# Own products paired with the routing, zero rows stored during the first aggregation, and the degrees' row made ahead of a branch, in a graph layer with experts

## Chip, cores and metric

One Trainium2 chip, of which the kernel uses one core. The metric is the device time in microseconds (us) of one execution. Before the change three executions took 2622.99, 2624.7 and 2629.7 us; the median is 2624.7 us.

## What is computed

`x` holds 6250 nodes of 256 features, `src` and `dst` hold 106,250 directed edges (50,000 drawn edges in both directions, and a loop for every node), sorted by `dst`. The reference, cut to what matters here:

```python
xn = layernorm(x)
def graph_conv(x, edges, W0, b0, W1, b1):        # every edge counts in both directions
    deg = maximum(segment_sum(ones, dst), 1)
    agg = segment_sum(x[src], dst) / deg[:, None]
    return x @ W0 + b0 + agg @ W1 + b1
h   = relu(graph_conv(xn, edges, W0_0, b0_0, W1_0, b1_0))     # 256 -> 512
gnn = graph_conv(h, edges, W0_1, b0_1, W1_1, b1_1)            # 512 -> 256
mix = linear_attention(xn, Wq, Wk, Wv, Wfc)   # k^T v per head, so one 256 x 256 matrix for all nodes
x   = x + gnn + mix
y   = layernorm(x)
top2, weights = top_k(y @ Wg + bg + bias, 2)                  # 8 experts
out = x + sum over the two experts e of weight * (relu(y @ W1[e] + b1[e]) @ W2[e] + b2[e])
```

Everything is float32 on the outside.

## The kernel before

**Tiling.** The nodes lie in `NB` = 49 blocks of 128. Four blocks are a group; there are `NGRP` = 13 groups, the last with one block. A neighbour sum is done as a product with an adjacency matrix: for each group of destination blocks and each source block `j`, a 128 x 512 tile of counts is multiplied with the normalized nodes `sent` (held in SBUF as two parts, a rounded one and the rest).

**Stages.** The kernel runs through five, one after the other; the times are those of the profiled execution.

1. 0 to 427 us: the edges are placed, that is, each edge gets a slot in a table `place` from which the adjacency tiles can be built by comparison. The nodes are normalized meanwhile.
2. 427 to 1172 us: the first aggregation (`aggregate`). VectorE makes one-hots (L667), TensorE multiplies them to adjacency tiles (L685), ScalarE takes these out of PSUM and adds up the degrees `degp` (L688), VectorE makes a bf16 copy `kept` (L695), SP stores it to `adjd` in DRAM (L696), and TensorE multiplies the tile with `sent` (L640). A unit is two tiles.
3. 1172 to 1190 us: the degrees are summed (L821), and the program takes a branch (`tc.If` at L727) that holds a slow path for edges which found no slot; with these inputs it isn't entered. Behind it, SP issues five loads (L860 to L862: transposed nodes and own products of group 0), and the row 1/degree is made: maximum and reciprocal (L864, L865), a transpose on TensorE (L867), a copy, a store of 24.5 KB to `rdeg_d` (L870). Then `mean(0)` reads it back, broadcast to all partitions (L877), and scales the aggregate `aggT` with it (L879).
4. 1190 to 1490 us: both dense products of the first convolution and the first part of the second.
5. From 1490 us: the second aggregation over the stored tiles with the gate behind each group, and from 2160 us the experts. These scatter and gather rows through the DRAM buffer `ybuf`, which has to be zero where no row is written.

**Order inside the first stage.** The order of TensorE's, VectorE's, ScalarE's and SP's instructions is that of the program text here (`manual_schedule`, L225): each of these engines works its own queue in order. Generators interleave the work. The main loop (L591) takes one batch `b` of four blocks (two pairs of blocks) after the other, 13 batches. In `assign(b)` a batch has

- ten rank groups: three matmuls (L380, L384, L389) into a PSUM tile `rk`, which VectorE reduces (L420); three tiles are in flight;
- a few small VectorE steps to `slot` (L439);
- for each of the two pairs, five `route` comparisons (L447) and four `carry` products (L456) on VectorE, with a yield behind each; then 38 routing matmuls (L469) and ScalarE's copies to `place` (L473 to L479), without a yield.

At each of its 31 yields, the batch advances `count(b + 1)` (the next batch's one-hots and running sums), `edges` (decoding of further edges), and, as long as a budget of `per_round` = 30 lasts, the generator `left`. `left` is the chain of `nodes(g)` for groups 2 to 12, and then `mixing()`. Groups 0 and 1 go first, ahead of the main loop (L579 to L583).

**`nodes(g)`** normalizes a group: statistics (L238, L241) on VectorE, a square root on ScalarE (`sd`, L246), its reciprocal on VectorE (L248), the normalization on ScalarE (L254) and the rounded part of `sent` (L257). Then eight transposes on TensorE (L264) give `xnT` (one buffer), which ScalarE copies out (L265) and stores to `xnT_d` (L267); VectorE subtracts for the second part of `sent` (L268). Next come the own products `xn @ W0_0`: four terms `f`, each of two matmuls (L273) into a PSUM tile `tp` (two buffers, shared with the transposes), an ACTIVATE with the bias (L276) and a store to `self_d` (L277), with a yield behind each term. The profile counts each float32 matmul as several records, so a term of a group of four blocks is four records of L273. Last comes `gram`, the sum of `xn^T xn` (L282), and the load of the group after the next (L286).

**`mixing()`** turns `gram` into the one 256 x 256 matrix of the attention. It begins with three weight loads on SP (L484) of which the first goes into `late`, the memory of the weights `W0_0` that the own products use, and a store of zeros to all of `ybuf` (L493, 13.4 MB in one DMA).

Of the kernel before, what the change touches and what calls it, by code (L numbers as in the profile page):

```python
# [8 lines left out]
F32 = mybir.dt.float32  # L9
# [3 lines left out]
AF = mybir.ActivationFunctionType  # L13
# [26 lines left out]
def tile_gps_layer(ctx: ExitStack, tc: tile.TileContext, a, out):  # L40
# [95 lines left out]
    with ExitStack() as p1:  # L136
# [90 lines left out]
        def load_nodes(g):  # L227
            load_rows(xns[g % XB][:, :, :D], blocks(g), nc.sync)

        def nodes(g):  # L230

            bs = blocks(g)
            n = len(bs)
            xn = xns[g % XB]
            st = wk.tile([P, T, nc.vector.BN_STATS_DIM], F32, name="st")
            mv = wk.tile([P, T, nc.vector.BN_AGGR_DIM], F32, name="mv")
            for i in range(n):
                nc.vector.bn_stats(st[:, i, :], xn[:, i, :D])  # L238
                yield
            for i in range(n):  # L240
                nc.vector.bn_aggr(mv[:, i, :], st[:, i, :])  # L241
                yield
            sd = wk.tile([P, T], F32, name="sd")
            rs = wk.tile([P, T], F32, name="rs")
            off = wk.tile([P, T], F32, name="off")
            nc.scalar.activation(sd[:, :n], mv[:, :n, 1], AF.Sqrt, bias=eps)  # L246
            yield
            nc.vector.reciprocal(rs[:, :n], sd[:, :n])  # L248
            yield
            nc.vector.scalar_tensor_tensor(off[:, :n], mv[:, :n, 0], -1.0, rs[:, :n], op0=OP.mult,  # L250
                                           op1=OP.mult)
            yield
            for i in range(n):
                nc.scalar.activation(xn[:, i, :D], xn[:, i, :D], AF.Identity, bias=off[:, i:i + 1],  # L254
                                     scale=rs[:, i:i + 1])
            part = sent[:, bs[0]:bs[-1] + 1]
            nc.scalar.copy(part[:, :, 0], xn[:, :n, :D])  # L257
            yield
            yield
            xnT = wk.tile([P, DC, T * P], F32, name="xnT", bufs=1)  # L260
            for c in range(DC):
                tp = pt1.tile([P, T * P], F32, name="tp")
                for i in range(n):
                    nc.tensor.transpose(tp[:, i * P:(i + 1) * P], xn[:, i, c * P:(c + 1) * P], ident)  # L264
                nc.scalar.copy(xnT[:, c, :n * P], tp[:, :n * P])  # L265
                yield
            nc.scalar.dma_start(xnT_d[:, :, bs[0] * P:(bs[-1] + 1) * P], xnT[:, :, :n * P])  # L267
            nc.vector.tensor_sub(part[:, :, 1], xn[:, :n, :D], part[:, :, 0].bitcast(F32))  # L268
            yield
            for f in range(FC):  # L270
                tp = pt1.tile([P, T * P], F32, name="tp")
                for c in range(DC):
                    nc.tensor.matmul(tp[:, :n * P], w00[:, c, f * P:(f + 1) * P],  # L273
                                     xnT[:, c, :n * P], start=(c == 0), stop=(c == DC - 1))
                own = (wq, wfc)[f % 2].rearrange("p c d -> p (c d)")
                nc.scalar.activation(own[:, :n * P], tp[:, :n * P], AF.Identity, bias=bh[:, f:f + 1])  # L276
                nc.scalar.dma_start(self_d[f, :, bs[0] * P:(bs[-1] + 1) * P], own[:, :n * P])  # L277
                yield

            for i, b in enumerate(bs):  # L280
                for c in range(DC):
                    nc.tensor.matmul(gram[:, GW[c]:GW[c] + W - c * P], xn[:, i, c * P:(c + 1) * P],  # L282
                                     xn[:, i, c * P:], start=False,
                                     stop=(b == NB - 1 and c == DC - 1))
                yield
            if g + XB < NGRP:  # L286
                load_nodes(g + XB)
# [125 lines left out]
        def assign(b):  # L413
# [25 lines left out]
            nc.vector.tensor_mul(flat(slot[:, :n]), rk, flat(fit))  # L439
            yield  # L440
            for i in range(n):
                routes = []
                for q0, q1 in QS:
                    nq = q1 - q0
# [36 lines left out]
        def mixing():  # L481


            for to, k in ((wkv, "WkvT"), (wq, "Wq"), (wfc, "WfcT")):  # L484
# [2 lines left out]
            x0, x1 = (xns[k].rearrange("p t w -> p (t w)") for k in range(2))  # L487
            b1p = x1[:, :NE * EC]
            nc.scalar.dma_start(b1p, a["b1e"].rearrange("p e c -> p (e c)"))

            none = x0[:, DC * W + D:DC * W + 2 * D]
            nc.vector.memset(none, 0.0)
            nc.sync.dma_start(ybuf.rearrange("(t p) d -> p t d", p=P),  # L493
                                            none[:, None, :].to_broadcast([P, TILES, D]))
            gs, m1 = (x0[:, :DC * n].rearrange("p (c d) -> p c d", c=DC) for n in (W, D))
            vk = x0[:, DC * W:DC * W + D].rearrange("p (c k) -> p c k", c=DC)
            gk, plain = x1[:, :DC * D].rearrange("p (c d) -> p c d", c=DC), x1[:1, DC * D:DC * D + 2 * D]
# [76 lines left out]
            for part in parts:  # L574
                yield from part

        EARLY = 2
        load_edges(PK * 2)
        for _ in nodes(0):  # L579
            pass  # L580
# [5 lines left out]
        for _ in count(0):  # L586
            pass
        load_edges(PK * 2)
        left = chained(*(nodes(g) for g in range(EARLY, NGRP)), mixing())
        per_round = -(-(NGRP - EARLY) * 30 // max(1, NBAT - 2))  # L590
        for b in range(NBAT):  # L591
            ahead_ = count(b + 1) if b + 1 < NBAT else iter(())
            k = b // (PK // PB) + 1
# [56 lines left out]
    def aggregate():  # L650

        with ExitStack() as s:
            hp = s.enter_context(tc.tile_pool(name="hots", bufs=4))
            ap = s.enter_context(tc.tile_pool(name="adj", bufs=4))
            pa = s.enter_context(tc.tile_pool(name="pa", bufs=4, space=PSUM))
            pg = s.enter_context(tc.tile_pool(name="pg", bufs=2, space=PSUM))
            s.enter_context(tc.manual_schedule(engines={ENG.PE, ENG.DVE, ENG.Activation}))
            hots, adjs, sums = {}, {}, {}
            units = [(g, js) for g in range(NGRP) for js in order_of(g)]

# [35 lines left out]
                nc.sync.dma_start(adjd[g, :, j, :n * P], kept[:, :n * P])  # L696

            AH, AB = 2, 1
            for u in range(len(units) + AH):
                if u < len(units):  # L700
                    g, js = units[u]
                    for j in js:
# [5 lines left out]
                if u >= AH:  # L708
# [8 lines left out]
                    if last:  # L717
                        n = len(blocks(g))
                        cols = slice(g * T * P, (g * T + n) * P)
                        nc.vector.tensor_copy(aggT[:, 0, cols], sums[g][0][:, :n * P])  # L720
                        nc.scalar.copy(aggT[:, 1, cols], sums[g][1][:, :n * P])

    def aggregate_any(first_conv):

# [2 lines left out]
        with tc.If(nc.values_load(misfit[0:1, 0:1], min_val=0, max_val=1) == 1), ExitStack() as s:  # L727
# [74 lines left out]
            for b in range(NB):  # L802
# [8 lines left out]
                else:  # L811
# [2 lines left out]
                    nc.vector.scalar_tensor_tensor(base, v[:, :D], rdeg[:, b:b + 1], base,  # L814
                                                   op0=OP.mult, op1=OP.add)
                    nc.sync.dma_start(btab[b * P:(b + 1) * P, :], base)
            if not first_conv:
                nc.vector.memset(rdeg, 0.0)

    aggregate()  # L820
    nc.vector.tensor_reduce(deg, degp, AX.X, OP.add)  # L821
    aggregate_any(True)
    ppool_ctx.__exit__(None, None, None)
    JL = 7
# [12 lines left out]
    with ExitStack() as p2:  # L837
# [22 lines left out]
        load_group(0)  # L860
        for f in range(FC):
            load_own(0, f)  # L862

        nc.vector.tensor_scalar(rdeg, deg, 1.0, None, op0=OP.max)  # L864
        nc.vector.reciprocal(rdeg, rdeg)  # L865
        pd = py.tile([P, 512], F32, name="pz")
        nc.tensor.transpose(pd[:NB, :P], rdeg, ident)  # L867
        rdT = wk.tile([P, T * P], F32, name="hT", bufs=6)[:NB, :P]
        nc.vector.tensor_copy(rdT, pd[:NB, :P])
        nc.sync.dma_start(rdeg_d.rearrange("(b p) -> b p", p=P), rdT)  # L870

        def mean(g):

            bs = blocks(g)
            cols = slice(bs[0] * P, (bs[-1] + 1) * P)
            rd = wk.tile([P, T * P], F32, name="rd", bufs=1)
            nc.sync.dma_start(rd[:, :len(bs) * P], bcast_rows(rdeg_d[cols], len(bs) * P))  # L877
            for c in range(DC):
                nc.vector.tensor_mul(aggT[:, c, cols], aggT[:, c, cols], rd[:, :len(bs) * P])  # L879

# [488 lines left out]
```

## Time and profile before

The profiled execution took 2623.89 us, of which 2622.1 us are the span from its first to its last instruction.

| | |
|---|---|
| median of three runs | 2624.7 us |
| profiled execution, its span | 2623.89 us, 2622.1 us |
| TensorE busy (matmuls) | 2418.6 us, 92% of the span |
| VectorE busy | 1605.2 us, 61% |
| ScalarE busy | 949.1 us, 36% |
| GpSimd busy | 343.5 us, 13% |
| granted TensorE clock, mean | 0.948 of full speed |
| DRAM traffic | 164.27 MB read, 159.95 MB written |

How such rows are read: "PE" is TensorE's matmuls, "PEld" its weight loads, "DVE" VectorE, "ACT" ScalarE, "SP" SyncE, which issues most of the DMAs; a "q" behind an engine's name is its queue of DMA issues, branches and the like. `L273` is line 273 of the kernel before. `tp<-xnT,late` says which tile is written from which. In a row of the timeline, the first number is the start and the second the duration in us, `x16` stands for 16 instructions of a kind in a row, and the bracket at the end gives how long the engine was idle before it and what ended that. In a list of waits, the waiting group stands left of the arrow and the one it waited for right of it.

### The profile page before, as it was taken

What the parts mean: (1) busy time and instruction counts of PE and PEld (TensorE: products, weight loads), DVE (VectorE), ACT (ScalarE), POOL (GpSimd) and SP (SyncE); (2) the same over time, 40 slices, a digit from 0 to 9 for tenths busy, and PEclk for the clock granted to TensorE, in tenths of its full rate; (3) what the DMA queues carried; (4) which work ended last, traced back from release to release, by engine and by line L of the source; (5) the groups of instructions that cost most, each with busy time, mean ns of one, the idle gap of its engine ahead of it and who ended that gap; (6) DMA issues with size and microseconds to landing.
All of it is one profiled execution on the core that took longest, in us unless ns stands there. A gap on an engine that the chain in (4) does not pass through costs nothing. (4 is left out here: it accounts for less than half of the span.)

```text
span 2622.1 us, 42322 instructions
## 1 busy us (share of the span) xinstructions
PE 2418.6 (92%) x13030; PEld 1828.8 (70%) x13030; DVE 1605.2 (61%) x4300; ACT 949.1 (36%) x2528; POOL 343.5 (13%) x372
## 2 busy tenths in 40 slices
PE   4788867999999999988999889999999968999998
PEld 2555545777777777776777778888888865777775
DVE  4888788888888888862333224444444434666666
ACT  2334313555555555541111123343343322333332
POOL 0000000000000000000000101211211212444444
PEclk9798877999999999998999999999999958999999
DMA  3222262333333333323333354554544442223333
GB/s 101 68 100 83 71 230 70 110 109 110 109 109 106 113 109 111 107 79 124 135 133 129 105 204 153 167 164 159 169 160 157 147 125 68 75 76 104 108 114 94
DMA packets 242754, 312.47 MB, mean 119 GB/s; under 512 B 53574, under 2 KB 202737, under 8 KB 242262
## 3 DMA queue, kind: packets, MB, share of 16 engines
q1 hardware_dynamic: 212690, 254.95, 30.3%
q0 software_dynamic: 16896, 33.80, 3.9%
q10 hardware_dynamic: 12932, 20.91, 2.2%
q8 instruction: 107, 1.75, 0.3%
q14 instruction: 129, 1.06, 0.1%
HBM read 164.27 MB, written 159.95 MB: 124 GB/s over the span
## 5 line engine op out<-in xcount | busy, mean ns | idle before, releaser
L640 PE MATMUL sum<-adj,sent 128*128 128x512 f32 (+1 forms) x5096 | 1258.2, 398 | 14.9 <-DVE adj L993 8.1
L640 PEld LDWEIGHTS sum<-adj,sent 128*128 128x128 f32 x5096 | 919.4, 193 | 194.2 <-DVE adj L993 8.5
L688 ACT ACTIVATE adj<-pt 128x512 fp32r<-128x512 f32 (+1 forms) x637 | 359.1, 570 | 348.5 <-PE pt L685 344.2
L667 DVE TENSOR_TENSOR oh<-iota,place 128x1024 bf16<-128x1024 bf16 (+1 forms) x686 | 404.1, 630 | 91.8 <-PE pt L685 89.7
L993 DVE CAST adj<-many 128x512 fp32r<-128x512 bf16 (+1 forms) x319 | 135.8, 427 | 321.8 <-PE sum L640 273.7
L991 ACT CAST adj<-many 128x512 fp32r<-128x512 bf16 (+1 forms) x318 | 188.6, 594 | 389.4 <-PE sum L640 346.8
L695 DVE CAST kept<-adj 128x512 bf16<-128x512 f32 (+1 forms) x637 | 235.9, 406 | 16.0 <-DMA adjd<-kept 6.9
L685 PEld LDWEIGHTS <-oh 128*128 128x128 bf16 x2548 | 148.1, 98 | 84.8 <-DVE kept L695 63.6
L1271 PEld LDWEIGHTS po<-w2e,hT 128*128 128x128 f32 x840 | 159.7, 190 | 67.3 <-issue 25.2
L685 PE MATMUL pt<-oh 128*128 128x128 bf16 x2548 | 204.7, 221 | 1.6 <-DVE oh L667 1.0
L1251 PE MATMUL pm<-w1e,yT 128*128 x420 | 201.3, 602 | 1.3 <-DMA row<-lists 1.3
L1271 PE MATMUL po<-w2e,hT 128*128 x840 | 198.6, 379 | 1.1 <-ACT hT L1263 1.1
L1275 ACT ACTIVATE res<-res,row 128x256 f32<-128x256 f32 x105 | 53.3, 508 | 301.6 <-DVE res L1274 301.6
L952 POOL IOTA home_i<- 128x8 int32 x1 | 0.1, 129 | 1063.6 <-SPq L727 1063.6
L1130 POOL DMA_INDIRECT lists<-rows,place_i x98 | 97.2, 992 | 305.9 <-DVE rows L1122 248.5
L1307 POOL DMA_INDIRECT out_dram<-both,at x105 | 106.8, 1017 | 175.2 <-DVE both L1305 165.9
L688 ACT ACTIVATION_READ_ACCUMULATOR adj<-pt 128x1 f32 x637 | 126.4, 198 | 0.0
L469 PE MATMUL rt<-carry,route 128*128 128x100 bf16 x931 | 68.5, 240 | 60.2 <-DVE carry L456 39.9
L1292 POOL DMA_INDIRECT got<-ybuf,at x105 | 108.2, 1031 | 69.3 <-issue 33.0
L1254 DVE TENSOR_TENSOR hb<-pm,b1c 128x512 f32<-128x512 f32 x105 | 72.6, 692 | 63.9 <-PE pm L1251 63.3
L1251 PEld LDWEIGHTS pm<-w1e,yT 128*128 128x128 f32 x420 | 72.7, 193 | 53.8 <-issue 52.0
L469 PEld LDWEIGHTS <-route 128*128 128x128 bf16 x931 | 61.3, 116 | 69.2 <-issue 59.0
(255 smaller groups left out, 2575.4 us busy)
## 6 DMA issues: line engine op xcount, KB each, us to landing
adjd<-kept SPq DMA_DIRECT2D x588, 128.0 KB, 1.8
many<-adjd SPq DMA_DIRECT2D x84, 896.0 KB, 4.6
row<-lists SPq DMA_DIRECT2D x105, 130.5 KB, 2.1
ybuf<-xn SPq DMA_DIRECT2D x1, 13440.0 KB
ybuf<-res SPq DMA_DIRECT2D x105, 128.0 KB, 2.0
hT<-self_d SPq DMA_DIRECT2D x48, 256.0 KB, 5.3
xn<-in_x_dram SPq DMA_DIRECT2D x12, 512.0 KB, 3.9
xnT_d<-xnT ACTq DMA_DIRECT2D x12, 512.0 KB, 3.2
```

What stands on the lines that cost most here:

```text
L469: nc.tensor.matmul(pl[:, r], routes[q // 4][:, q % 4, :, r], carry[:, q - q0, :, :, r], start=(q == 0), stop=(q == Q - 1))
L640: nc.tensor.matmul(sums[g][c][:, :n * P], sent[:, j, k, c * P:(c + 1) * P], adj[:, :n * P], start=(first and k == 0), stop=(last and k == 1))
L667: nc.vector.tensor_tensor(oh, iota2[:, None].to_broadcast([P, m, P, 2]), place[:, j, v0:v0 + m, None, :].to_broadcast([P, m, P, 2]), op=OP ...
L685: nc.tensor.matmul(cols, o[:, :, r], o[:, :, 1 - r], start=(m == 0), stop=(m + 1 == len(todo)))
L688: nc.scalar.activation(adj[:, :n * P], pt[:, :n * P], AF.Copy, accum_out=degp[:, j, g:g + 1])
L695: nc.vector.tensor_copy(kept[:, :n * P], adjs[g, j][:, :n * P].bitcast(F32))
L991: nc.scalar.copy(adj[:, :n * P], from_)
L993: nc.vector.tensor_copy(adj[:, :n * P], from_)
L1251: nc.tensor.matmul(pm, yT[:, c], w1e[:, bass.ds(e, 1), c, :].rearrange("p o f -> p (o f)"), start=(c == 0), stop=(c == DC - 1))
L1271: nc.tensor.matmul(po, hT[:, f], w2e[:, bass.ds(e, 1), f, :].rearrange("p o d -> p (o d)"), start=(f == 0), stop=(f == EC - 1))
L1292: ga = nc.gpsimd.indirect_dma_start(out=gots[t % 4], out_offset=None, in_=ybuf, in_offset=bass.IndirectOffsetOnAxis(ap=outs[t][1][:, 0:1], ...
L1307: st = nc.gpsimd.indirect_dma_start(out=out, out_offset=bass.IndirectOffsetOnAxis(ap=at[:, 1:2], axis=0), in_=both, in_offset=None, bounds ...
```

## The change

Four edits.

1. **Own products.** `nodes(g)` no longer multiplies a group's own products. It puts its four terms into a queue `owed`; `own_term` takes one term out and issues its matmuls, its ACTIVATE and its store. `assign` calls it twice ahead of each pair of blocks, so four times a batch. Since `xnT` has one buffer, terms that are still owed are done ahead of the next group's transposes. Groups 0 and 1 put in nothing; a new generator `first_terms`, which runs behind the last group and ahead of `mixing`, loads their `xnT` back from `xnT_d` over SP, one group after the other, and does their terms. As a group now has four yields fewer, `per_round` goes from 30 to 26.
2. **Zero rows.** The memset and the one store of 13.4 MB in `mixing` are gone. The first aggregation has a tile of zeros (memset on GpSimd) and stores it 105 times, 128 KB each, at every third unit until all rows are done, over SP. SP's order is now the program's in this stage too.
3. **Degrees.** The row 1/degree is made and stored by a function `degrees()` ahead of the branch (and once more at the end of the branch's slow path), and the broadcast for group 0 is loaded there, to a tile `rd0`. All later groups load into the same tile.
4. The pools: `rd0` is in the pool of `aggT`; the transpose's PSUM and SBUF tiles are in pools of their own inside `degrees()`.

```diff
+        EARLY = 2
+        owed = []
+        def own_term():
+            if not owed:
+                return
+            g, f, xnT = owed.pop(0)
+            bs = blocks(g)
+            n = len(bs)
+            tp = pt1.tile([P, T * P], F32, name="tp")
+            for c in range(DC):
+                nc.tensor.matmul(tp[:, :n * P], w00[:, c, f * P:(f + 1) * P],
+                                 xnT[:, c, :n * P], start=(c == 0), stop=(c == DC - 1))
+            own = (wq, wfc)[f % 2].rearrange("p c d -> p (c d)")
+            nc.scalar.activation(own[:, :n * P], tp[:, :n * P], AF.Identity, bias=bh[:, f:f + 1])
+            nc.scalar.dma_start(self_d[f, :, bs[0] * P:(bs[-1] + 1) * P], own[:, :n * P])
+        def first_terms():
+            for g in range(EARLY):
+                while owed:
+                    own_term()
+                    yield
+                bs = blocks(g)
+                xnT = wk.tile([P, DC, T * P], F32, name="xnT", bufs=1)
+                nc.sync.dma_start(xnT[:, :, :len(bs) * P], xnT_d[:, :, bs[0] * P:(bs[-1] + 1) * P])
+                owed.extend((g, f, xnT) for f in range(FC))
+                yield
+            while owed:
+                own_term()
+                yield
 ...
         def nodes(g):
 ...
+            while owed:
+                own_term()
             xnT = wk.tile([P, DC, T * P], F32, name="xnT", bufs=1)
 ...
-            for f in range(FC):
-                tp = pt1.tile([P, T * P], F32, name="tp")
-                for c in range(DC):
-                    nc.tensor.matmul(tp[:, :n * P], w00[:, c, f * P:(f + 1) * P],
-                                     xnT[:, c, :n * P], start=(c == 0), stop=(c == DC - 1))
-                own = (wq, wfc)[f % 2].rearrange("p c d -> p (c d)")
-                nc.scalar.activation(own[:, :n * P], tp[:, :n * P], AF.Identity, bias=bh[:, f:f + 1])
-                nc.scalar.dma_start(self_d[f, :, bs[0] * P:(bs[-1] + 1) * P], own[:, :n * P])
-                yield
+            if g >= EARLY:
+                owed.extend((g, f, xnT) for f in range(FC))
 ...
             for i in range(n):
+                for _ in range(FC // PB):
+                    own_term()
                 routes = []
 ...
-            none = x0[:, DC * W + D:DC * W + 2 * D]
-            nc.vector.memset(none, 0.0)
-            nc.sync.dma_start(ybuf.rearrange("(t p) d -> p t d", p=P),
-                                            none[:, None, :].to_broadcast([P, TILES, D]))
 ...
-        left = chained(*(nodes(g) for g in range(EARLY, NGRP)), mixing())
-        per_round = -(-(NGRP - EARLY) * 30 // max(1, NBAT - 2))
+        left = chained(*(nodes(g) for g in range(EARLY, NGRP)), first_terms(), mixing())
+        per_round = -(-(NGRP - EARLY) * 26 // max(1, NBAT - 2))
 ...
+            none = s.enter_context(tc.tile_pool(name="none", bufs=1)).tile([P, D], F32, name="none")
+            nc.gpsimd.memset(none, 0.0)
-            s.enter_context(tc.manual_schedule(engines={ENG.PE, ENG.DVE, ENG.Activation}))
+            s.enter_context(tc.manual_schedule(engines={ENG.PE, ENG.DVE, ENG.Activation, ENG.SP}))
 ...
+            every = len(units) // TILES
             for u in range(len(units) + AH):
+                if u % every == 0 and u // every < TILES:
+                    t = u // every
+                    nc.sync.dma_start(ybuf[t * P:(t + 1) * P, :], none)
 ...
+    rd0 = apool.tile([P, T * P], F32, name="rd0")
+    def degrees():
+        nc.vector.tensor_scalar(rdeg, deg, 1.0, None, op0=OP.max)
+        nc.vector.reciprocal(rdeg, rdeg)
+        with tc.tile_pool(name="rdT", bufs=1) as sb, tc.tile_pool(name="pdT", bufs=1, space=PSUM) as ps:
+            pd = ps.tile([P, P], F32, name="pd")
+            nc.tensor.transpose(pd[:NB, :P], rdeg, ident)
+            rdT = sb.tile([P, P], F32, name="rdT")
+            nc.vector.tensor_copy(rdT[:NB], pd[:NB])
+            nc.sync.dma_start(rdeg_d.rearrange("(b p) -> b p", p=P), rdT[:NB])
+        n = len(blocks(0)) * P
+        nc.sync.dma_start(rd0[:, :n], bcast_rows(rdeg_d[:n], n))
 ...
     nc.vector.tensor_reduce(deg, degp, AX.X, OP.add)
+    degrees()
     aggregate_any(True)
 ...
-        nc.vector.tensor_scalar(rdeg, deg, 1.0, None, op0=OP.max)
-        nc.vector.reciprocal(rdeg, rdeg)
-        pd = py.tile([P, 512], F32, name="pz")
-        nc.tensor.transpose(pd[:NB, :P], rdeg, ident)
-        rdT = wk.tile([P, T * P], F32, name="hT", bufs=6)[:NB, :P]
-        nc.vector.tensor_copy(rdT, pd[:NB, :P])
-        nc.sync.dma_start(rdeg_d.rearrange("(b p) -> b p", p=P), rdT)
         def mean(g):
 ...
-            rd = wk.tile([P, T * P], F32, name="rd", bufs=1)
-            nc.sync.dma_start(rd[:, :len(bs) * P], bcast_rows(rdeg_d[cols], len(bs) * P))
+            rd = rd0
+            if g:
+                nc.sync.dma_start(rd[:, :len(bs) * P], bcast_rows(rdeg_d[cols], len(bs) * P))
```

More of the change, by code (lines that the diff above doesn't have):

```diff
@@ L575, in chained @@
                 yield from part
-        EARLY = 2
         load_edges(PK * 2)
@@ L816, in aggregate_any @@
                     nc.sync.dma_start(btab[b * P:(b + 1) * P, :], base)
-            if not first_conv:
+            if first_conv:
+                degrees()
+            else:
                 nc.vector.memset(rdeg, 0.0)
@@ L821, in tile_gps_layer @@
     nc.vector.tensor_reduce(deg, degp, AX.X, OP.add)
+    degrees()
     aggregate_any(True)
```

## The prediction

> **What bounds the kernel now.** I read the busy time by stretch first, then VectorE's waits in the first stretch, then three places of the timeline. By stretch (length, then busy us of TensorE, its weight loads, VectorE, ScalarE, GpSimd, then granted clock, DMA share, GB/s):
>
> ```profile
> 0.00:427.00 427.00, 301.63 (x1886) 194.83 (x1886) 322.02 (x805) 128.10 (x414) 4.22 (x11) 0.83 0.31 100
> 427.00:1172.00 745.00, 742.50 (x5097) 579.62 (x5096) 616.46 (x1338) 394.52 (x1291) 2.49 (x3) 1.00 0.33 109
> 1172.00:1190.00 18.00, 0.42 (x1) 0.16 (x1) 1.79 (x6) 0.00 (x0) 0.00 (x0) 0.56 0.51 153
> 1190.00:1490.00 300.00, 298.45 (x1188) 225.48 (x1188) 103.28 (x188) 49.46 (x101) 0.00 (x0) 0.99 0.34 115
> ```
>
> From 427 on TensorE has no gap to give (742.5 of 745, 298 of 300), but for 18 us between the first aggregation and the first convolution. The stretch to 427, which places the edges, is VectorE's: 322 us busy, and 20 to 25 us of every 27 in the batches. Its idle time there is what a new order can win or lose (us in all, times, longest):
>
> ```profile
> DVE route L447 <- PE rt L469: 25.1, 12, 6.8
> DVE rank L420 <- PE rk L389: 22.9, 14, 5.0
> DVE tmp L318 <- DMA eds<-in_src_dram: 16.2, 1, 16.2
> DVE sent L268 <- ACT sent L257: 7.5, 8, 2.3
> DVE xn L529 <- ACT xn L525: 6.7, 1, 6.7
> ```
>
> So from 48 to 427 VectorE waits some 80 us, mostly for TensorE's ranks and routes. The timeline shows how own products cause it in batch 0: sixteen matmuls of L273 from 78.62, then gram, and only at 88.59 the routing whose operands were ready at 82.6; the next batch of route tiles then waits 6.85 us for their buffers.
>
> ```profile
> 78.62 8.83 PE L273 MATMUL tp<-xnT,late 128*128 128x512 f32 x16 [0.23 <-ACT xnT L265]
> 88.59 1.04 PE L469 MATMUL rt<-carry,route 128*128 128x100 bf16 x19
> 90.72 0.69 DVE L447 TENSOR_TENSOR route<-iota,slot 128x1024 bf16<-128x1024 bf16 x1 [6.85 <-PE rt L469]
> ```
>
> **Startup: -7.8 us.** The 16.2 us wait:
>
> ```profile
> 35.34 13.45 SPq L74 DMA_DIRECT2D xn<-in_x_dram  x2
> 63.18 0.32 DVE L318 TENSOR_SCALAR tmp<-eds 128x304 int32<-128x304 int32 x1 [16.25 <-DMA eds<-in_src_dram]
> ```
>
> SP stands in the load of xn for group 3 until gram of group 1 ends (45.58 + 2.79 = 48.4); the 16 edge loads behind it are issued from 49.6 to 61.5, and VectorE waits for the last. Gram of group 1 stands behind that group's own products (38.6 to 45.7). With these gone it follows the transposes (end 37.8) and ends at 40.6, 7.8 us earlier; SP and VectorE follow by as much, since VectorE is idle from 46.9.
>
> **Batches 0 to 7: about -4 us.** In a warm run the sixteen matmuls of a group (L273) take 7.13 us, so two of its four terms are 3.5 us; eight transposes or the gram of a group 2.8, three ranks 1.3, the routing of a pair 2.8. VectorE needs some 8.5 us from the last rank to a pair's carries, 6 for the second pair's. I laid the changed queues out batch by batch with these:
> - Batch 0: ahead of the first routing stand only transposes and gram (5.6 us), so it starts when its carries are ready. Of 6.85 us about 1 stays: -5.8.
> - Ranks no longer have own products between them: the rank waits of batches 2, 3, 4, 7 and 8 (0.8, 4.2, 2.5, 5.6, 5.0 us) mostly go. But a term not yet done must go ahead of the next group's transposes, and where these fall between ranks and routing (batches 1, 3, 4, 6), as much is ahead of the routing as before: two terms flushed, transposes, gram, two terms: 12 to 13 us against 8.5. Waits of 3 to 5 us stay.
> - A new wait, which the before does not have. The terms ahead of a second pair stand behind the first pair's routing on TensorE, and their ACTIVATEs behind both on ScalarE. Behind these ACTIVATEs stands the next group's `sd` (batches 1 and 4), for which VectorE's reciprocal waits ahead of the third route. That is 3.5 + 0.7 + 0.3 + about 0.2 us after the routing ended, where the route would have gone on 0.8 us before its end: about 5.5 us in batch 1, 4.3 in batch 4. In batches 3 and 6 the normalization waits likewise behind the first pair's ACTIVATEs, and L268's subtraction with it, 3 us each, mostly in place of a route wait.
> - By batch, before to after: b1 2.7 to 8.6, b2 3.7 to 3.2, b3 5.2 to 6.4, b4 9.6 to 8.0, b5 2.7 to 1.7, b6 3.7 to 4.9, b7 6.8 to 3.0 (with the ranks it delays into b8). Sum +1.4, with batch 0 -4.4.
>
> **The two groups put last, batch 8: +18 us.** Now, after the last group's small terms (four at 128 columns), the mixing follows:
>
> ```profile
> 325.05 2.63 PE L273 MATMUL tp<-xnT,late 128*128 128x128 f32 x16
> 327.71 0.39 SPq L485 DMA_DIRECT2D late<-in_WkvT_dram  x1
> 338.80 1.06 PE L469 MATMUL rt<-carry,route 128*128 128x100 bf16 x19
> 339.51 0.41 DVE L529 SCALAR_TENSOR_TENSOR xn<-bkv,xn 1x256 f32<-1x256 f32 x1 [6.74 <-ACT xn L525]
> ```
>
> From the last term's end (327.7) it takes 11.8 us until VectorE goes on, the reload of `late` among them. In the changed queue the small terms end earlier, between the ranks (by 325.0); then SP loads xnT of group 0 (its single buffer is free only now), TensorE waits, three ranks and four terms follow, then the same for group 1. A load of 512 KB lands in 3.9 us (xn; 5.2 for xnT where the DMA is busier; 3.2 for a store of that size). So 325.0 + 3.9 + 1.3 + 7.1 + 4.0 + 7.1 = 348.4, in place of 327.7: VectorE waits 20.7 us longer, as its next instruction is the mixing's and the routing stands behind it. The rank wait at the batch's start (5.0) is counted with batch 7 above: it goes, so +15.7.
> Here a rule of the Trainium skill speaks against the change: "TensorE: Matmul & The Clock Gate", "The HAM clock gate (the "warmup" mystery)", has the clock at half after an idle window of about 3.4 us, and full only after as much work. The row of a warm group says 7.13; the group at 78.62, where the clock granted from 78 to 88 was 0.80, took 8.83. Two loads of 4 us would make two cold starts of 1.7 us: +19.1. No row shows a term group after so long a stop; I take +18, ends +11 (loads of 2.5 us, warm) and +24.
>
> **Zero rows: +0.5 us.** The store of 13.4 MB at 333 keeps DMA 0.99 busy to 375, but nothing waits for it: taking it out, and its memset (0.27), wins nothing. The 105 stores of 128 KB cost SP 0.32 us each (L696's median), 34 us where SP issues 637 x 0.32 = 204 of 745. The work that hides them: kept tiles have 4 buffers at 2 per 2.4 us unit, so 4.8 us to reuse, less 0.4 of copy, some 0.9 of issue and
>
> ```profile
> adjd<-kept SPq DMA_DIRECT2D x588, 128.0 KB, 1.8
> ```
>
> to landing: 1.7 us to spare, and VectorE is 0.4 us idle a unit. A zero store ahead adds its issue and 13.4 MB / 42 us = 0.4 us of transfer: 0.7. Only in the last group (one block, 1 us units) VectorE waits already (most of L695's 6.9 us for this DMA), and five zero stores fall there: 0 to +2 us. Without the spare, each further 0.1 us would cost 10 us in all.
>
> **Degrees ahead of the branch: -9 us.** Matmuls of the aggregation end at 1171.13, the convolution starts at 1190.29:
>
> ```profile
> 1175.11 0.19 DVE L864 TENSOR_SCALAR rdeg<-deg 128x49 f32<-128x49 f32 x1 [2.97 <-DVEq L727]
> 1180.17 0.36 SPq L870 DMA_DIRECT2D rdeg_d<-hT  x1
> 1184.61 0.35 SPq L877 DMA_DIRECT2D rd<-rdeg_d  x1
> 1189.29 1.29 DVE L879 TENSOR_TENSOR aggT<-aggT,rd 128x512 f32<-128x512 f32 x2 [11.97 <-DMA rd<-rdeg_d]
> ```
>
> The row is stored behind five loads (1.5 MB) and read back behind them. In the new order: degrees reduced at 1171.95, 0.19 + 0.47, transpose and copy to 1173.6; SP's last adjacency store ends at 1173.7; 24.5 KB stored without loads ahead, 2 to 3 us, to 1176.5; 256 KB read, 2.5 to 3.5, to 1179.8. SP then takes the branch (2.5 us from compare to its first event now) and waits there for the landing: 1180. Multiply, 0.65, and TensorE starts near 1181: 9 us saved, 6.5 to 10.5. What is late next are the own and xnT loads, now behind the row: from 1181, landed within 7 us as now (1177.4 to 1184.6), when the last of four products is only ready at 1190. The pause stays above the clock's window, so the slow first matmuls stay. The second branch has no such row, and all later stretches have the same instructions.
>
> **Sum:** -7.8 - 4.4 + 18 + 0.5 - 9 = -2.7 on the profiled execution (span 2622.1, 2623.9 with what lies around it): 2621. The median of the runs is 0.8 higher; I say 2622. A measurement here can tell about 0.3%, 7.9 us, so this is no change.
>
> **Rivals.**
> 1. Faster: the three gains whose place and size the trace fixes (7.8, 5.8, 9: 22.6) stand, and the losses are oversized: loads land in 2.5 us on a quiet queue (-6 with warm clock) and the ScalarE waits overlap route waits (-8). For it: DMA is 0 to 0.3 busy there. Against: both waits are in program order. 2608.
> 2. Slower by the in-order queues: flushed terms hold ScalarE in more batches than I counted, as two PSUM buffers tie each term to the ACTIVATE of the second before it. 2 us more in six batches and the top of batch 8's range: +18: 2639. Against: nothing of it shows now, with the same two buffers.
> 3. Slower by the zero stores: if one delays landings by more than 1.7 us, kept stalls VectorE and then TensorE in the aggregation; 2.0 us would give 105 x 0.3 = 31: 2653. Against: 0.7 estimated.
> 4. The reordering does nothing: flushes bring as many waits as they take; only the boundary is won: 2615.
>
> **How the numbers follow.** Forecast (no change) 0.44; rival 1 0.22, rival 4 0.12, rival 2 0.16, rival 3 0.06. Faster 0.34, same 0.44, slower 0.22. My own sum is good to 8 us (batch 8 from -7 to +6, waits 4, boundary 2); to leave out two in ten I go to 2606 and 2639.
>
> **What would show it.** L318's long wait down to 8.5 us; the batch 0 route wait near 1; reciprocal (L248's line) waiting for sd some 5 us in two batches; one stall of VectorE of near 30 us around the two loads; aggregation still 742 of 745 busy; the boundary 10 us. Wrong if the loads cost TensorE nothing, if VectorE's idle time before the aggregation falls under 80 us, or if kept waits for its DMA in every group.

## The result, and the profile after

The changed kernel is slower: 2635.87 us against 2623.27 us, medians of 20 runs each. The ratio is 1.0044 with a 95% interval of 1.0032 to 1.0056, so 8.4 to 14.7 us. The prediction had 2622 us and no change as the likeliest case; the time lies inside its range of 2606 to 2639 us, on the side that it had called the less likely.

The profiled execution took 2633.13 us, its span is 2631.4 us, 9.3 more than before. The busy time by stretch shows where they are. The columns are length, then busy us of TensorE, its weight loads, VectorE, ScalarE and GpSimd, the granted clock, DMA share and GB/s. The stretches of the kernel after are placing, the twelve wide groups of the first aggregation, its last group of one block, the pause at the branch, and the first convolution:

```profile
0.00:443.40 443.40, 300.44 (x1886) 196.41 (x1887) 321.88 (x806) 128.93 (x417) 4.54 (x12) 0.83 0.21 68
443.40:1160.33 716.93, 716.93 (x4853) 554.21 (x4853) 597.08 (x1240) 379.40 (x1191) 2.49 (x3) 1.00 0.39 129
1160.33:1197.99 37.66, 35.78 (x248) 35.04 (x246) 21.00 (x100) 15.91 (x95) 0.00 (x0) 0.71 0.24 58
1197.99:1205.03 7.04, 0.22 (x3) 0.03 (x1) 1.29 (x3) 0.27 (x1) 0.00 (x0) 0.50 0.20 51
1205.03:1505.00 299.97, 298.97 (x1188) 225.35 (x1188) 102.68 (x187) 49.52 (x101) 0.00 (x0) 0.99 0.36 123
```

The kernel before split its aggregation in the same way:

```profile
427.63:1144.55 716.92, 716.92 (x4852) 554.43 (x4853) 596.74 (x1239) 378.45 (x1191) 2.49 (x3) 1.00 0.33 111
1144.55:1171.13 26.58, 25.56 (x247) 25.18 (x245) 18.22 (x96) 15.34 (x95) 0.00 (x0) 1.00 0.27 59
```

Placing ends 15.8 us later (443.40 for 427.63). The wide groups take the same time to 0.01 us, with the zero rows beside them. The last group takes 11.1 us more (37.66 for 26.58), at a mean clock of 0.71. The pause at the branch is 12.1 us shorter (7.04 for 19.16). What lies behind is 5.4 us shorter, between the first product of the second aggregation and the last matmul of the gate (657.4 us for 662.8); the other profiles, of either kernel and of the experiments, lie between 657 and 666 us there, so this is within their scatter. 15.8 + 11.1 - 12.1 - 5.4 = 9.4.

**Placing.** VectorE's waits from 48 us on, in the kernel after (us in all, times, longest):

```profile
DVE xn L554 <- ACT xn L550: 33.7, 1, 33.7
DVE route L477 <- PE rt L499: 19.0, 10, 3.4
DVE rs L281 <- ACT sd L279: 14.0, 4, 8.2
DVE sent L303 <- ACT sent L290: 10.4, 7, 4.5
DVE tmp L346 <- DMA eds<-in_src_dram: 9.6, 1, 9.6
DVE rank L448 <- PE rk L417: 8.1, 6, 3.0
```

Ranks, routes and startup wait 64.2 us before and 36.7 us now. Against that stand the new waits for `sd`, and one of 33.7 us in the mixing. Its place on the timeline:

```profile
309.74 15.96 SPq L256 DMA_DIRECT2D xnT<-xnT_d  x2
314.02 3.75 PE L242 MATMUL tp<-xnT,late 128*128 128x512 f32 x4 [4.42 <-DMA xnT<-xnT_d]
...
319.82 5.34 PE L242 MATMUL tp<-xnT,late 128*128 128x512 f32 x12
...
329.82 8.80 PE L242 MATMUL tp<-xnT,late 128*128 128x512 f32 x16 [4.66 <-DMA xnT<-xnT_d]
...
338.65 0.40 SPq L515 DMA_DIRECT2D late<-in_WkvT_dram  x1
...
351.79 0.41 DVE L554 SCALAR_TENSOR_TENSOR xn<-bkv,xn 1x256 f32<-1x256 f32 x1 [33.71 <-ACT xn L550]
```

TensorE stands idle for two reloads, 4.42 and 4.66 us. The terms behind them take 9.09 and 8.80 us, where a group of terms at full clock took 7.13; the granted clock was 0.51 from 314.0 to 319.8 and 0.81 from 329.8 to 338.7. Ranks lie between them, and then come the 13.1 us of the mixing that were 11.8 before.

**The last group.** At 1176.73 VectorE has waited 2.01 us for a store of `kept` to land; TensorE waits 1.72 us for the one-hots behind that, and from then on eight products take 1.95 us in place of 1.09:

```profile
1174.40 1.09 PE L664 MATMUL sum<-adj,sent 128*128 128x128 f32 x8
...
1176.73 0.23 DVE L721 CAST kept<-adj 128x128 bf16<-128x128 f32 x1 [2.01 <-DMA adjd<-kept]
...
1177.21 0.49 PE L711 MATMUL pt<-oh 128*128 128x128 bf16 x2 [1.72 <-DVE oh L693]
...
1177.46 1.95 PE L664 MATMUL sum<-adj,sent 128*128 128x128 f32 x8
```

The granted clock from 1177 to 1198 is 0.50, with TensorE busy for 20.79 of these 21 us. The kernel before has a shorter pause in the same place, and its products stay at 1.09 us:

```profile
1161.04 0.43 PE L685 MATMUL pt<-oh 128*128 128x128 bf16 x2 [1.02 <-DVE oh L667]
1161.28 1.09 PE L640 MATMUL sum<-adj,sent 128*128 128x128 f32 x8
```

**The branch.** The degrees' row is out of the way of the loads:

```profile
1198.56 0.32 SPq L765 DMA_DIRECT2D rdeg_d<-rdT  x1
1200.10 0.34 SPq L767 DMA_DIRECT2D rd<-rdeg_d  x1
1204.02 1.29 DVE L920 TENSOR_TENSOR aggT<-aggT,rd 128x512 f32<-128x512 f32 x2 [5.50 <-SPq L773]
```

From the issue of the store to the multiplication it is 5.5 us. The loads behind are issued from 1204.97, and the first `hT` of the convolution has landed by 1209.80, while TensorE is busy for 9.97 of the first 10 us.

### The profile page after: what moved, and what is told of

The parts are those of the page before. It is cut to its first block, busy times and chain, and to the rows that moved or that the text cites. A ratio compares the mean times of both kernels' runs of the same rounds, so it can differ in the third digit from the quotient of the medians.

```text
span 2631.4 us, 42419 instructions
## 1 busy us (share of the span) xinstructions
PE 2422.8 (92%) x13030; PEld 1833.1 (70%) x13030; DVE 1604.8 (61%) x4299; ACT 950.5 (36%) x2528; POOL 344.4 (13%) x373
```

## Experiments

The theory after these profiles: (a) the reloads of groups 0 and 1 make the placing late; (b) the zero rows in the last group make it pause, and the pause costs the clock. Rivals: the placing is late for the place of the mixing, not the loads; the clock falls by chance, or because narrow matmuls lose it anyway.

**Zero rows done before the last group.** The changed kernel stores at units 0, 3, ... 312, the last five in the last group (units 300 to 324).

```diff
-            every = len(units) // TILES
+            every = 2
```

> The changed kernel with its 105 stores of zero rows at every second unit in place of every third, so that all are done before the last group of the first aggregation (units 300 to 324) begins. Theory: the five stores in the last group delay the landing of kept, VectorE and TensorE pause, the clock falls to half and stays there, because that group's matmuls are narrow. Then the last group falls from 37.7 us to the 26.6 of the kernel before, the first twelve stay at 716.9, and the whole takes 2635.9 - 11 = 2625 us. Rival: the fall of the clock is chance, or the load of the stores in general: 2636 as the changed kernel, or more, since the stores are closer together (each kept landing 0.2 us later would give 105 x 0.2 = 21: 2657).

Ratio to the kernel before 1.0009 (0.9999 to 1.0018), 9 us under the changed kernel, near the 11 of the theory. But the profile does not show what the theory said: this last group also falls to half the clock, after a pause of 0.74 us and two more units, and takes 33.3 us, not 26.6.

```profile
1170.75 0.43 PE L711 MATMUL pt<-oh 128*128 128x128 bf16 x2 [0.74 <-DVE oh L693]
1170.99 1.09 PE L664 MATMUL sum<-adj,sent 128*128 128x128 f32 x8
...
1173.10 1.95 PE L664 MATMUL sum<-adj,sent 128*128 128x128 f32 x8
```

So the fall isn't the zero rows' alone, and how often it happens had to be seen.

**Groups 0 and 1 queue their own terms first.**

```diff
-            if g >= EARLY:
-                owed.extend((g, f, xnT) for f in range(FC))
+            owed.extend((g, f, xnT) for f in range(FC))
 ...
-            for g in range(EARLY):
-                while owed:
-                    own_term()
-                    yield
-                bs = blocks(g)
-                xnT = wk.tile([P, DC, T * P], F32, name="xnT", bufs=1)
-                nc.sync.dma_start(xnT[:, :, :len(bs) * P], xnT_d[:, :, bs[0] * P:(bs[-1] + 1) * P])
-                owed.extend((g, f, xnT) for f in range(FC))
-                yield
```

> The changed kernel, but groups 0 and 1 queue their own terms like all others, and nothing is loaded back ahead of the mixing. Theory: the two reloads and the eight terms between them are what VectorE's wait of 33.7 us holds; it falls to near 7, the startup keeps most of its 6.6 us gain, and batch 0 gives back some 7, because group 1's four terms again stand ahead of its first routing. Placing takes 443.4 - 23 + 7 = 427, the whole 2635.9 - 16 = 2620 us. Rival: the mixing is late for another reason (its own chain shifted to a worse place among the ranks, or the terms ahead of pairs): the wait stays over 20 us and the whole is 2636 + 7 = 2643.

Ratio 0.9955 (0.9943 to 0.9967): 11.8 us faster than before, 8 us better than expected. The long wait falls from 33.7 to 6.2 us, and placing ends at 420.31. Two details of the expectation were wrong: the startup gain is lost whole (16.2 us again), as group 0's ACTIVATEs now stand behind group 1's normalization on ScalarE; and batch 0 gives back 4.1 us, not 7 (32.0 us to the next batch's first rank, 27.9 in the changed kernel and 34.8 before; its route wait is 4.03 us).

**The degrees alone,** on the kernel before, with `degrees()` and `rd0` as in the change:

```diff
     nc.vector.tensor_reduce(deg, degp, AX.X, OP.add)
+    degrees()
     aggregate_any(True)
 ...
-        nc.sync.dma_start(rdeg_d.rearrange("(b p) -> b p", p=P), rdT)
 ...
+            rd = rd0
+            if g:
+                nc.sync.dma_start(rd[:, :len(bs) * P], bcast_rows(rdeg_d[cols], len(bs) * P))
```

> The kernel before, with only the degrees' row made ahead of the branch. Theory: the pause of TensorE between the aggregation and the convolution falls from 19.2 us to 7, and nothing behind it is late: 2623.3 - 12 = 2611 us. Rival: the five loads, now behind the row, make the convolution wait, or the gain is given back at the next boundary: 2618 to 2623.

Ratio 0.9964 (0.9952 to 0.9977): 9.4 us faster, for 12 expected. The pause is 6.9 us. The last group fell to half the clock in this profile too (33.7 us), without any zero rows.

**Own products alone,** on the kernel before, with `own_term` and `first_terms` as in the change:

```diff
+            if g >= EARLY:
+                owed.extend((g, f, xnT) for f in range(FC))
 ...
+                for _ in range(FC // PB):
+                    own_term()
                 routes = []
 ...
-        left = chained(*(nodes(g) for g in range(EARLY, NGRP)), mixing())
-        per_round = -(-(NGRP - EARLY) * 30 // max(1, NBAT - 2))
+        left = chained(*(nodes(g) for g in range(EARLY, NGRP)), first_terms(), mixing())
+        per_round = -(-(NGRP - EARLY) * 26 // max(1, NBAT - 2))
```

> The kernel before, with only the own products queued ahead of the pairs' routing and those of groups 0 and 1 last. Theory: the placing stage ends 15.8 us later, as in the changed kernel's profile, and all else stays: 2639 us. Rival, the prediction's own sum for these parts (-7.8 - 4.4 + 18 = +5.8): 2629 us, the rest of the 15.8 being due to the other parts (the 13.4 MB store that is gone from the mixing) or to chance.

Ratio 1.0036 (1.0023 to 1.0049): 9.4 us slower, 6.0 to 12.9. Placing ends at 438.46. The changed kernel's other profile (below) gives 442.7, and two experiments with the same placing 438.5 and 441.7; six profiles with the placing of the kernel before have 427.0 to 430.2. So the loss in the profiles is some 13 us (means of 441 and 428), at the upper end of what the times show, and 3 us of the first profile's 15.8 are scatter. The measured time lies between the two theories.

**Zero rows alone,** on the kernel before, with the tile `none`, `every` and SP's order as in the change:

```diff
-            nc.sync.dma_start(ybuf.rearrange("(t p) d -> p t d", p=P),
-                                            none[:, None, :].to_broadcast([P, TILES, D]))
 ...
+                if u % every == 0 and u // every < TILES:
+                    t = u // every
+                    nc.sync.dma_start(ybuf[t * P:(t + 1) * P, :], none)
```

> The kernel before, with only the zero rows stored in the first aggregation (the changed kernel's way, every third unit, five of them in the last group). Theory: the twelve wide groups stay at 716.9 us; the last, narrow group, which takes 26.6 us where the clock holds and 33.3 to 33.8 where it falls late (three profiles so far without these stores), takes 36.6 to 37.7, as the two profiles with them show. So +4 us at least, up to +11 if the kernel before mostly keeps its clock: 2624 + 4 to 11, a ratio of 1.0015 to 1.004. Rival, the prediction's term: +0.5 us, a ratio of 1.0002.

Ratio 1.0026 (1.0014 to 1.0038): 6.8 us slower. The rival's 1.0002 is outside. The twelve wide groups take 716.9 us again, the last 37.7:

```profile
429.34:1146.27 716.93, 716.93 (x4852) 554.19 (x4853) 596.53 (x1240) 378.86 (x1191) 2.49 (x3) 1.00 0.39 129
1146.27:1183.94 37.67, 35.69 (x247) 34.99 (x246) 20.35 (x98) 15.97 (x95) 0.00 (x0) 0.71 0.25 59
```

The three parts alone add up to 9.4 + 6.8 - 9.4 = 6.8 us, where the whole change measures 12.6. Each is good to some 3 us, so the difference of 5.8 is inside the noise.

**Eight buffers for kept, zero rows as they were.**

```diff
-                kept = ap.tile([P, T * P], BF16, name="kept")
+                kept = ap.tile([P, T * P], BF16, name="kept", bufs=8)
```

> The changed kernel with eight buffers for the kept tiles in place of four, zero rows as they were. Theory: what pauses TensorE in the last group is VectorE's wait for a kept tile's landing; with eight buffers nothing waits, the clock stays full, and the last group takes 26 to 27 us for 37.7, so 11 us less than the changed kernel: 2625, a ratio of 1.0002 to the kernel before. Rival: narrow matmuls fall to half the clock with or without a pause[...]: the group stays at 33 us or more, ratio 1.002 to 1.0045.

Ratio 1.0003 (0.9993 to 1.0013): 10.7 us under the changed kernel. Wide groups, last group and pause at the branch:

```profile
441.66:1157.29 715.63, 715.63 (x4853) 553.20 (x4853) 596.09 (x1239) 378.88 (x1191) 2.49 (x3) 1.00 0.39 130
1157.29:1183.20 25.91, 25.84 (x247) 25.24 (x245) 19.49 (x97) 15.49 (x95) 0.00 (x0) 1.00 0.32 77
1183.20:1192.83 9.63, 0.29 (x2) 0.16 (x2) 2.21 (x7) 0.27 (x1) 0.00 (x0) 0.62 0.21 57
```

The same narrow matmuls, with the same zero rows, keep the clock through 25.9 us when TensorE doesn't pause. VectorE still waits 3.7 us for landings here, but TensorE pauses for 0.06 us only. So narrow matmuls don't lose the clock by themselves; it is the pause, which the wait for a buffer of `kept` brings.

**Eight buffers in the kernel before.**

> The kernel before with eight kept buffers. Theory: its own last group falls to half the clock in most executions, and its profiled execution was one of those that didn't; then the buffers win some 5 of the 7 us: a ratio of 0.998. Rival: the last group of the kernel before is 26.6 us as a rule, and the fall belongs to the changed kernels: a ratio of 1.000.

Ratio 0.9994 (0.9984 to 1.0003): the last group takes 25.3 us; no change that can be told apart from the noise. The 5 us expected are outside the interval, which ends at 4.2 us. The waits alone are worth 1.3 us (26.6 to 25.3), so, as an estimate, a fall worth 7 us can come in at most four of ten executions of the kernel before ((4.2 - 1.3) / 7): it mostly keeps its clock.

**The kernel before twice more, the changed one once more.**

> The kernel before, profiled again, to see how often its last group of the first aggregation falls to half the clock: 26.6 us if it holds, as in the first profile, 33 to 34 us if it falls, as in three experiments that have the same stage. With equal chances of both, the theory that the zero stores make a certainty of a chance stands; two profiles that hold speak for it too.

> As the run before it, a third profile of the kernel before: 26.6 us or 33 to 34 us for the last group.

> The changed kernel, profiled again. Theory: its last group falls to half the clock again and takes 36 to 38 us; the placing ends at 438 to 439 us, as in two experiments that have the same stage, the 443.4 of its first profile having some 5 us of chance in it. Rival: the group takes 27 us, so the 11 us were chance; and the placing ends at 443.

The kernel before kept its clock both times, and the changed one lost it again. Placing in the latter ended at 442.7 us, as the rival had it.

The last group of the first aggregation in all profiles with four buffers:

| zero rows in the group | kernels | its length, us | fell to half the clock |
|---|---|---|---|
| none | before, three profiles | 26.6, 26.4, 26.1 | no |
| none | zero rows early, degrees alone, own products alone | 33.3, 33.7, 33.8 | yes, late |
| five | after, two profiles | 37.7, 37.8 | yes |
| five | zero rows alone, own terms first, both reloads ahead (below) | 37.7, 36.6, 35.7 | yes |

With the five stores TensorE's longest pause is 1.4 to 2.0 us, and the clock fell in five of five. Without them it is 0.5 to 1.0 us, and the clock fell in three of six. Among the latter, 0.74 us was followed by a fall and 1.02 us was not, so the length of the pause alone doesn't decide.

The traces' records of the clock show what else does. In all these profiles the clock changes only on a grid of 3.413 us: stretches of 727.04, 740.69, 34.13 and 20.48 us at one clock are 213, 217, 10 and 6 such steps. So each pause can be divided by the borders of the steps. Within the step at whose end the clock fell, TensorE was idle for 0.97, 1.02, 1.25, 1.67 and 1.39 us in the five profiles with zero rows in the group, and for 0.74, 0.51 and 0.99 us in the three without. In the three that kept the clock, a border cut the pause of 1.02, 0.82 or 0.53 us, and no step had more than 0.67 us of it. But for the 0.51 us (the degrees alone, whose step before had 0.66), falling and keeping part between 0.67 and 0.74 us. If that holds, the clock falls behind a pause of some 1.5 us wherever it lies (an estimate: cut in two, one piece has at least 0.74), and behind a shorter one or not by where the border meets it. This is read from eleven profiles; no run moved a pause on purpose, and the one exception stays open.

**Both reloads ahead.** The rows of groups 0 and 1 go into the two buffers of normalized rows, free by then, so that neither load waits for terms.

```diff
-                while owed:
-                    own_term()
-                    yield
                 bs = blocks(g)
-                xnT = wk.tile([P, DC, T * P], F32, name="xnT", bufs=1)
+                xnT = xns[1 - g].rearrange("p t w -> p (t w)")[:, :DC * T * P]
+                xnT = xnT.rearrange("p (c n) -> p c n", c=DC)
```

> The changed kernel, with xnT of groups 0 and 1 both loaded back ahead of group 12's terms, into the two buffers of the normalized rows, which are free by then; the terms stay where they were, eight in a row ahead of the mixing. Theory: TensorE's two waits for these loads (4.4 and 4.7 us) go, and of the cold terms behind them (3.8 + 5.3 and 8.8 us in place of 7.1 each) some 3 us: VectorE's long wait falls from 32 to 34 us to near 21, and the whole by 10 us to 2625, a ratio of 1.0005. Rival: the loads hardly matter, as the terms in a row and the load of late behind them are what the mixing waits for: a wait of 28 us or more, ratio 1.003 or more.

Ratio 0.9996 (0.9986 to 1.0005): 12.6 us under the changed kernel. Placing ends at 426.46, and the wait is as expected:

```profile
DVE xn L551 <- ACT xn L547: 21.1, 1, 21.1
```

This settles (a): the same terms in the same place make the placing no longer than that of the kernel before (427.0 to 430.2) once TensorE doesn't stand still for their operands; the granted clock over them, from 311.0 to 326.4 us, is 1.00. The rest of the wait, the eight terms in a row, is about paid for by startup and batch 0.

**A better version:** terms of groups 0 and 1 also two ahead of each pair, zero rows early, eight buffers.

```diff
+            while owed:
+                own_term()
+                yield
             for g in range(EARLY):
-                while owed:
-                    own_term()
-                    yield
 ...
                 owed.extend((g, f, xnT) for f in range(FC))
-                yield
-            while owed:
-                own_term()
-                yield
+                while owed:
+                    yield
 ...
-            every = len(units) // TILES
+            every = 2
 ...
-                kept = ap.tile([P, T * P], BF16, name="kept")
+                kept = ap.tile([P, T * P], BF16, name="kept", bufs=8)
```

> The changed kernel with three edits: the terms of groups 0 and 1 also go two ahead of each pair (each group's xnT is loaded back as soon as the buffer is free, and the mixing follows behind them, one or two batches later); zero rows at every second unit; eight kept buffers. Theory: startup and batch 0 keep their 13 us, batch 8 no longer holds loads and terms in a row, and the placing ends near 420 us where the changed kernel needs 438 to 443; with the degrees 12 us less and a last group of 26.6 us the whole takes 2624 - 7 - 12 - 5 = 2600 us, a ratio of 0.991. Rival: the mixing, moved to later batches, which had little beside them, costs there what batch 8 wins: placing 430 or more, 2610 us, 0.995.

2605.22 us, ratio 0.9921 (0.9903 to 0.9939): faster than both kernels. Placing, wide groups, last group and pause:

```profile
0.00:422.20 422.20, 292.13 (x1886) 191.78 (x1887) 321.55 (x806) 128.41 (x417) 4.54 (x12) 0.85 0.23 72
422.20:1137.70 715.50, 715.50 (x4852) 553.06 (x4853) 596.04 (x1239) 378.82 (x1191) 2.50 (x3) 1.00 0.39 130
1137.70:1162.96 25.26, 25.26 (x247) 25.13 (x245) 20.62 (x97) 15.36 (x95) 0.00 (x0) 1.00 0.28 62
1162.96:1171.00 8.04, 0.29 (x2) 0.15 (x2) 2.14 (x7) 0.27 (x1) 0.00 (x0) 0.68 0.20 58
```

VectorE's wait in the mixing is 3.4 us. The rival had something: one wait for ranks of 7.5 us appears in batch 10, where the mixing now lies, and this batch takes 38.1 us for 21.9 before. Batches 8 to 10 together take 88.7 us, 83.8 in the kernel before and 77.5 where groups 0 and 1 queue their own terms first. So what this version wins at the start against that one (the first rank of batch 1 at 84.4 for 95.2) it gives back there, and its placing is no shorter (422.20 for 420.31, one profile each). It is some 9 us faster than that one, about what the last group differs by (25.3 us for 36.6); putting groups 0 and 1 off isn't shown to pay.

## Why the prediction was wrong

By its own terms, from the first rank of each batch in the two first profiles (63.42 and 56.85 in batch 0, 98.26 and 84.77 in batch 1, 309.81 and 299.87 in batch 8, 347.30 and 359.59 in batch 9):

| term | predicted, us | first profiles, us |
|---|---|---|
| startup | -7.8 | -6.6 |
| batch 0 | -5.8 | -6.9 |
| batches 1 to 7 | +1.4 | +3.6 |
| batch 8, two groups last | +18 | +22.2 |
| batches 9 to 12 | 0 | +3.5 |
| zero rows | +0.5 | +11.1 |
| degrees | -9 | -12.1 |
| all behind | 0 | -5.4 |
| sum | -2.7 | +9.4 |

**The step that failed** is "Only in the last group (one block, 1 us units) VectorE waits already (...), and five zero stores fall there: 0 to +2 us." The place and the wait were right, and so was the cover in the wide groups: 105 stores cost them nothing. Wrong was the price. The prediction priced a late landing at its own length; what it costs is the clock. A pause of 1.7 us brought 20.8 us at half speed, as the rows from 1174.40 on show, and the group took 11.1 us more. In time this is 6.8 us for the zero rows alone, and 10.7 us that eight buffers take off the changed kernel.

The prediction weighed the clock for the two reloads and for the pause at the branch, not here. "TensorE: Matmul & The Clock Gate", "The HAM clock gate (the "warmup" mystery)", in the Trainium skill, was about right for the reloads (9.09 and 8.80 us, so 2.0 and 1.7 above the warm 7.13). For the last group the rule itself would have misled: it asks for an idle window of some 3.4 us, and gives full speed back after as much sustained work. Here a pause of 1.72 us sufficed, and 0.74 us in another profile; and 20.8 us of work at 99% busy gave nothing back. The measurement decides.

**The second miss, of size,** is batch 8 and what follows: +25.7 for +18. The mechanism was right: VectorE behind the mixing, the mixing behind two reloads. From the end of the small terms to the end of group 1's terms it took 29.0 us (309.6 to 338.6), where the prediction's chain has 23.4 (325.0 to 348.4): 9.1 us of loads for 7.9, 2.3 of ranks for 1.3, 17.9 of terms for 14.2 warm (the pieces overlap by 0.3). The mixing also ran into batch 9, where it cost 3 us of waits for ranks; the prediction had nothing there. Some 3 us of the placing are scatter, as repeated profiles show; own products alone measure +9.4 us, where the prediction's sum for these parts is +5.8, just under the interval.

**Right:** startup and batch 0; batch 1 (+5.7 for +5.9, with the reciprocal's wait behind its own ACTIVATEs: 8.2 us for 5.5, and less elsewhere); and the degrees, -9.4 us in time for -9. The pause came out shorter than predicted only where the last group ran at half the clock, since the row is then made beside the slow last products: 6.9 to 7.5 us there, 8.0 and 9.6 where the clock held, against some 10 predicted.

Of the rivals, the one on the landings of `kept` (2653 us, 6 in 100) named the right wait, in every group rather than the last, and without the clock. The one on in-order queues (2639 us) gives nearly the time by luck: the flushed terms cost little more than had been counted.

## What to carry to other kernels

Where a stage's matmuls get narrow at its end, its buffers are recycled faster too: look there for waits that the wide part hides, and price a pause not by its length alone but by what may be left of the stage at half the clock. A few more buffers for the tile that waits were the cheap cure here: with eight the clock held in three of three profiles, while with the zero rows stored earlier it still fell. And work put off to the end of a stage should have its operands loaded before it gets there: two loads of 4.5 us each on an idle TensorE cost 12.6 us here, as waits and as the matmuls at a lower clock behind them.

## What the hardware did that was not expected

The late landing in the last group is no accident of one run. It comes some 16 us into the group in every profile with four buffers. Two to three microseconds before the wait ends, one packet of an instruction queue (`q8`) starts to move, and the stores to `adjd` trickle at some 10 GB/s for half a microsecond or more. In the kernel before, DMA from 1157 to 1162 us (40 slices of 0.125 us):

```profile
GB/s 0 31 180 51 0 57 170 19 0 98 140 139 0 145 99 2 6 158 133 6 6 12 23 10 12 10 0 0 0 0 0 0 0 0 0 0 2 168 92 0
...
q8 instruction: 1, 0.02, 1.1%
```

The same pair, one packet of 0.02 MB and a tail of some 10 GB/s, is there in every profile with four buffers. The packets come about every 19 us of the aggregation, and the wide groups show the same: of the 147 stores to `adjd` whose landing the trace of the kernel before records there, nine took over 2.5 us, and eight of these had a `q8` packet in flight, against 14 of the other 138. So the two go together; that the packet holds up the store was not tested. The Trainium skill says that an engine's instructions come in blocks over its own DMA queue and that this is mostly hidden ("Runtime: NRT & Kernel Launch", "Instruction fetch mechanics"); if these belong together, this is a place where it isn't hidden, as a single store of 32 KB is awaited by a ring of four buffers.
